# Projections of queries, keys and values by seven products of quarters, in steps on two shared PSUM banks

## The chip, the cores and the metric

The kernel runs on one core of a Trainium2 chip. Its metric is the device time of one execution in microseconds (us), the median of several. All arithmetic is in 32-bit floats. PE is the matrix engine, DVE the vector engine, ACT the scalar engine, POOL the GpSimd engine, SP the engine whose queue issues the DMAs.

## What is computed

Two blocks follow each other on 4 batches of 1024 rows of 512 features. The first is a graph attention over 20 neighbours. The second, which the change is in, is a transformer block with modulation by a condition vector:

```python
mod = silu(c) @ W_mod + b_mod
sh_msa, sc_msa, g_msa, sh_mlp, sc_mlp, g_mlp = split(mod, 6)
x = x + g_msa * attention(modulate(layernorm(x), sh_msa, sc_msa), W_qkv, W_out, b_out)
x = x + g_mlp * ff(modulate(layernorm(x), sh_mlp, sc_mlp), W1, b1, W2, b2)
```

`attention` projects the 512 features to queries, keys and values of 16 heads of 64, takes a softmax over all 1024 rows of the batch, and projects back with `W_out`. `ff` goes to 2048 hidden features, through an exact gelu, and back.

## The kernel before, in words

**Three stages.** The graph block runs first, over 32 tiles of 128 rows. Then the attention runs in 256 slots: 4 batches of 8 pairs of heads (`gp`) of 8 tiles of query rows. Then comes the feed-forward block. All instructions are issued in the order in which the program writes them, so each engine's queue is in program order.

**What a slot is.** Slot s handles one tile of 128 query rows for one pair of heads. Its fixed part is written first: `turn(s-1, 0)` (DVE transposes the weights of the slot before, in blocks of 32, into `wd`), `scores` (PE: four products, psc in two tiles of two PSUM banks), `largest` (DVE: the row maximum of both heads), `weights` (ACT: exponentials of both heads, with their sums), `scaled(0)` (ACT: first head's weights by the reciprocal of their sum), `turn(s-1, 1)`, `scaled(1)` (POOL: the second head's weights). After the fixed part, `emit(s, s+1)` writes what the planner has put into slot s, the fill. So on ACT every copy of the fill stands behind both exponentials and `scaled(0)` of the same slot, and on DVE every operation of the fill stands behind both maxima. The next slot's scores stand on PE behind the whole fill.

**The fill.** A list of entries `(lo, hi, units, place, function)`: a first and a last slot, a load of PE in units, and a place inside the slot. `attend` (weights times values for 256 queries, 2 units, place 1), the projections, `project` (1 unit, the product with `W_out`, added into the row by DVE) and `gates_of` (place 2), `norm_T` (transposes of normalised rows, place 3), and works of other engines without load. The planner starts each entry at its first slot and moves entries one by one to the slot of least load in their window while that lowers the load.

**The projections of before.** `mm_qk(b, gp, k, n, half)` makes half of a product of a [512 x 128] weight and the 512 x 512 half `n` of a batch's rows: two matmuls of 128x128 by 128x512. `mm_v(b, g, n)` makes 128 rows of values for a group of four heads: four matmuls of 128x128 by 128x256. Results go through four PSUM banks in turn (`MM`), which `attend`, `project`, `norm_T` and `gates_of` use too; ACT copies them to `qT`, `kT` (with its columns in another order) and `vt`. A matmul of 32-bit floats is two instructions in the profile. No projection waits in its slot for a copy that another entry of that slot has made.

**DMA.** `turn` on an odd slot issues four DMAs of 256 KB on SP's queue, which carry the tile `wd` (two slots' transposed weights of one head, two buffers per head) to `wT`.

**seven.** The feed-forward block already multiplies its quarters by seven products in place of eight (`seven`, `sums_a`, `sums_b`), on four banks. One of its units (`first`) is spread over the last slots of the attention, one step a slot.

Of the kernel before, what the change touches and what calls it, by code (L numbers as in the profile page):

```python
# [41 lines left out]
def cond_block_kernel(  # L42
# [49 lines left out]
    sel = cst.tile([P, B, P], F32, name="sel")  # L92
    for k in range(4):
        q = slice(32 * k, 32 * k + B)
        nc.vector.tensor_copy(sel[q], ident[q, q].unsqueeze(2).to_broadcast([B, B, P]))
# [23 lines left out]
    def spread(k, b, pg):  # L119

        q = slice(32 * k, 32 * k + B)
        nc.tensor.matmul(pg, lhsT=sel[q, b, :], rhs=gates[q, :], start=True, stop=True)
        return pg
# [6 lines left out]
    with ExitStack() as gctx:  # L130
# [16 lines left out]
        with ExitStack() as sctx:  # L147
# [58 lines left out]
            for b in range(B):  # L206
                pr = sps.tile([P, F], F32, name="pr", tag="s")
                nc.tensor.matmul(pr, lhsT=sel[:B, b, :], rhs=qrows, start=True, stop=True)
                evac(b, qrB[:, b, :], pr)
# [173 lines left out]
        def load_w(held, key, tag, src, cols):  # L383

            t = rp.tile([P, FC, 2, P], F32, name=tag, tag=tag, bufs=2)
            for k, col in enumerate(cols):
                nc.sync.dma_start(t[:, :, k, :], src[:, col : col + P].rearrange("(c p) f -> p c f", p=P))
            held[key] = t
# [58 lines left out]
        def seven(get, opens, short, lhs, rhs, nk, room, done):  # L447
# [5 lines left out]
            a, b, c, d, s5 = ({} for _ in range(5))  # L453

            def product(t, which, fresh):
                for q in range(2):
                    for k in range(nk):
                        nc.tensor.matmul(  # L458
                            t[:, q * HB : (q + 1) * HB],
                            lhsT=lhs(which, q, k),  # L460
                            rhs=rhs(which, k),
                            start=(fresh and q == 0 and k == 0),
                            stop=(k == nk - 1),
                            skip_group_check=True,
                        )

            def bank_of(held, name):
                held[0] = get(name)
                if opens and name in ("mb", "md"):
                    nc.tensor.matmul(held[0], lhsT=ident, rhs=hT[1, 0][:, 0, :], start=True, stop=True)  # L470
                return held[0]

            def step0():
                product(bank_of(a, "ma"), 0, True)
                nc.scalar.copy(bank_of(b, "mb"), a[0])  # L475

            def step1():
                product(bank_of(c, "mc"), 4, True)
                s5[0] = short()
                nc.scalar.copy(s5[0], c[0])  # L480

            def step2():
                product(b[0], 5, False)
                nc.vector.tensor_tensor(bank_of(d, "md"), b[0], s5[0], ALU.add)

            def step3():
                product(a[0], 1, False)
                done(0, 0, a[0])

            def step4():  # L490
                product(b[0], 6, False)
                s6 = room()
                nc.vector.tensor_tensor(s6, b[0], s5[0], ALU.add)
                done(1, 1, s6)

            def step5():
                product(d[0], 2, False)
                done(0, 1, d[0])

            def step6():  # L500
                product(b[0], 3, False)
                done(1, 0, b[0])

            return step0, step1, step2, step3, step4, step5, step6
# [3 lines left out]
        ex, hs, hx, tx = {}, {}, {}, {}  # L508

        def mlp_rows():  # L510

            h = hT[1, 0]
            if not tx:
                tx[0] = rp.tile([P, FC, VB * P], F32, name="tx", tag="hT", bufs=2)
            o = [tx[0][:, k, :].rearrange("p (c r) -> p c r", c=2) for k in range(3)]
            sums_b(nc.gpsimd, o, h[:, :2, :HB], h[:, :2, HB:], h[:, 2:, :HB], h[:, 2:, HB:])

        def mlp_weights(e, i, home):

            ex[i] = home()  # L520
            o = [ex[i][:, k * HB : (k + 1) * HB].rearrange("p (c f) -> p c f", c=2) for k in range(3)]
            w = w1g[i]
            sums_a(e, o, w[:, :2, 0, :], w[:, 2:, 0, :], w[:, :2, 1, :], w[:, 2:, 1, :])

        def up_lhs(p):
            def lhs(which, q, c):
                i = 2 * p + q
                at = {4: 0, 5: 1, 2: 2}.get(which)
                if at is not None:
                    return ex[i][:, at * HB + c * P : at * HB + (c + 1) * P]  # L530
                h, f = {0: (0, 0), 1: (0, 1), 3: (1, 1), 6: (1, 0)}[which]
                return w1g[i][:, 2 * f + c, h, :]

            return lhs

        def up_rhs(which, c):
            at = {4: 0, 5: 1, 3: 2}.get(which)
            if at is not None:
                return tx[0][:, at, c * HB : (c + 1) * HB]
# [253 lines left out]
        for s in range(-4, NTA + 2):  # L793
# [44 lines left out]
            if s == 25:  # L838
# [3 lines left out]
                load_v(0, 1)  # L842
# [5 lines left out]

    vp = ctx.enter_context(tc.tile_pool(name="vp", bufs=1, side="right", reuse_waits="tile"))
# [4 lines left out]
    with ExitStack() as actx:  # L854
        ap_ = actx.enter_context(tc.tile_pool(name="ap", bufs=1, reuse_waits="tile"))
        MM = dict(tag="mm", bufs=4)
# [45 lines left out]
        def mm_v(b, g, n):  # L902

            if (b, g) not in vt:
                vt[b, g] = vp.tile([P, NT, GW], F32, name="v", tag="v", bufs=2)
            if n % 2 == 0:
                part["v", n // 2] = ps.tile([P, 2, GW], F32, name="pvv", **MM)
            pt = part["v", n // 2]
            for c in range(FC):
                nc.tensor.matmul(  # L910
                    pt[:, n % 2, :],
                    lhsT=hT[0, 2 * b + n // VB][:, c, n % VB * P : (n % VB + 1) * P],
                    rhs=wv[b, g][:, c].rearrange("p k f -> p (k f)"),
                    start=(c == 0),
                    stop=(c == FC - 1),
                )
            if n % 2 == 1:
                nc.scalar.copy(vt[b, g][:, n - 1 : n + 1, :], pt)

        def attend(b, gp, k):  # L920
# [13 lines left out]
            if p == 0 and k == 0:  # L934
                oT[b, g] = op_.tile([P, 2, S], F32, name="oT", tag="oT", bufs=2)
            nc.scalar.copy(
                oT[b, g][:, p, k * QB : (k + 1) * QB].rearrange("p (t u q) -> p u t q", t=QT, u=4),
# [3 lines left out]
        def project(b, g, n):  # L941

            po = ps.tile([P, F], F32, name="pout", **MM)
            for p in range(2):
                nc.tensor.matmul(  # L945
                    po,
                    lhsT=oT[b, g][:, p, n * P : (n + 1) * P],
# [45 lines left out]
        def turn(b, gp, t, j):  # L993

            k, at = divmod(t, QT)
            if at == 0:
                wd[j] = ap_.tile([P, 4 * KC, QT, U], F32, name="wd", tag=f"wd{j}", bufs=2)
# [28 lines left out]

        def add(lo, hi, units, place, f, *args):
            fill.append((lo, hi, units, place, lambda: f(*args)))

        for b in range(B):  # L1030
            s0 = b * NP * NT
            for gp in range(NP):
                g, p = divmod(gp, 2)
                at = s0 + gp * NT
                if gp == 0 and b > 0:
                    for h, (ld, rws, tr) in enumerate(
                        ((-18, (-15, -14, -13, -12), -11), (-10, (-9, -9, -8, -8), -7))
# [6 lines left out]

                if at > 0:
                    for k in range(2):
                        for n in range(2):
                            for half in range(2):

                                lo = at - (8 if gp > 0 else (9, 5)[n])  # L1050
                                add(lo, at - (2 if gp < NP - 1 else 4), 1, 2, mm_qk, b, gp, k, n, half, bank)
                if p == 0:
                    for n in range(NT):
                        lo, hi = (at - 12, at + 1) if g > 0 else (max(at - (9, 5)[n // VB], 0), at + 3)
                        add(lo, hi, 1, 2, mm_v, b, g, n)
# [4 lines left out]
                if p == 1:  # L1060
                    for n in range(NT):
                        lo = at + QT * (NB - 1) + LAG + (3 if g == 0 else 2)
                        add(lo, lo + (7 if g == NGRP - 1 else 10), 1, 2, project, b, g, n)
# [11 lines left out]
                if at - 16 >= 0:  # L1075
                    add(at - 16, at - 16, 0, 0, load_qk, b, gp)
                if p == 0 and at - 24 >= 0:
                    add(at - 24, at - 24, 0, 0, load_v, b, g)
# [3 lines left out]
        add(NS - 18, NS - 18, 0, 0, norm_load, 1, 0)  # L1082
# [4 lines left out]
        for i, at in enumerate((NS - 14, NS - 11, NS - 13, NS - 12)):  # L1087
            add(at, at, 0, 0, load_w1, i, "wqk" if i < 2 else "wv")
        add(NS - 7, NS - 7, 0, 4, mlp_rows)
        for i in range(2):  # L1090
            add(NS - 9 + i, NS - 9 + i, 0, 4, mlp_weights, nc.gpsimd, i, home_q(("qT", "kT")[i]))

        def short():
            return op_.tile([P, F], F32, name="s", tag="s", bufs=2)
# [10 lines left out]
        first = seven(bank, True, short, up_lhs(0), up_rhs, 2, room0, done0)  # L1105
        for k, f in enumerate(first):
            at = NS - 7 + k
            add(at, at, (1.5, 1, 1.5, 1, 1, 1, 1)[k], 2, f)
# [3 lines left out]
        used = {}  # L1112
        for w, f in zip(where, fill):
            used[w] = used.get(w, 0) + f[2]
        moved = True
        while moved:
            moved = False
            for k, (lo, hi, units, _, _) in enumerate(fill):
                to = min(range(lo, hi + 1), key=lambda s: used.get(s, 0) - (units if s == where[k] else 0))
# [233 lines left out]
```

## Time and profile before

| | |
|---|---|
| median of three runs | 3174.8 us (3174.73 to 3180.2) |
| the profiled execution | 3184.05 us, of which the span from first to last instruction is 3182.3 us |
| PE busy | 3142.3 us, 99% of the span |
| DVE, ACT, POOL busy | 61%, 44%, 33% |
| graph block | first 457 us |
| attention slots | 457 us to 2350 us, 7.4 us a slot on average |
| feed-forward block | from 2390 us to the end |
| mean granted PE clock | 0.993 |

Busy time of PE is modelled from the start and the size of each matmul, and matmuls overlap in it, so a mean duration in a group is longer than the distance between two of them: busy time divided by the count is nearer to that distance. A line such as `L409 PE MATMUL pqk<-hT,wqk ... x1024 | 475.1, 604 | 0.0` gives the busy time, the mean of one instruction in ns, and the idle time of the engine before the group.

### The profile page before, as it was taken

The page shows a single profiled execution, that of the slowest core. Times are in us where ns is not written, and L with a number is a line of the kernel's source. Part 1 is how long each engine was busy: PE and PEld are TensorE (multiplying, and loading weights), DVE is VectorE, ACT ScalarE, POOL GpSimd, SP SyncE. Part 2 cuts the span into 40 slices and gives each one's busy share as a digit, 9 for nine tenths or more (in the row PEclk, how much of TensorE's full clock was granted, in tenths as well). Part 3 has the DMA queues.
Part 4 walks back from the last instruction along what each step waited for, and adds up shares of the span by engine and source line. Part 5 has one row for each costly group of instructions (what it writes and reads, how often), then busy time and mean ns, then how long its engine had stood idle before and what let it go on. Part 6 is the DMA issues. An engine that isn't in the chain of part 4 may idle for free.

```text
span 3182.3 us, 39273 instructions
## 1 busy us (share of the span) xinstructions
PE 3142.3 (99%) x14571; PEld 1938.9 (61%) x14571; DVE 1941.9 (61%) x2718; ACT 1406.2 (44%) x2312; POOL 1066.0 (33%) x580
## 2 busy tenths in 40 slices
PE   8999999999999999999999999999999999999999
PEld 5666665544444544454544454544457888888888
DVE  2688866777767777767777767777864332223222
ACT  1344446555555555555555555555641221112211
POOL 1344325344343544343544343544432101111020
PEclk8999999999999999999999999999999999999999
DMA  4233317776777776777776777776862101101010
GB/s 164 71 102 98 119 45 184 160 177 153 175 170 180 177 177 154 175 170 180 178 177 154 176 171 179 178 176 147 193 162 88 40 27 40 40 14 40 27 40 14
DMA packets 272850, 405.29 MB, mean 127 GB/s; under 512 B 24660, under 2 KB 97424, under 8 KB 272660
## 3 DMA queue, kind: packets, MB, share of 16 engines
q1 hardware_dynamic: 272660, 402.78, 50.6%
q8 instruction: 116, 1.90, 0.2%
q14 instruction: 74, 0.61, 0.1%
HBM read 109.08 MB, written 25.17 MB: 42 GB/s over the span
## 4 chain that ended last, share of the span: by engine, by line
PE 86%; DVE 5%; SPq 2%; DMA 2%; issue 2%; POOL 2%; ACT 1%; POOLq 0%; DVEq 0%; ACTq 0%
PE psc L965 14%; PE pqk L409 14%; PE pav L927 12%; PE pvv L910 7%; PE pout L945 6%; PE mbd L458 5%; PE mbu L458 5%; PE mad L458 3%; PE mau L458 3%; PE pa L647 2%; PE pf L607 2%; PE mcd L458 2%; PE mdd L458 2%; SPq L1004 2%; PE mdu L458 2%
## 5 line engine op out<-in xcount | busy, mean ns | idle before, releaser
L991 POOL TENSOR_SCALAR w<-w,sm 128x1024 f32<-128x1024 f32 x256 | 730.5, 2853 | 1074.3 <-DVE sm L987 1074.3
L982 ACT ACTIVATE w<-psc,mx 128x1024 f32<-128x1024 f32 x512 | 570.7, 1115 | 769.3 <-DVE mx L976 768.8
L976 DVE TENSOR_REDUCE mx<-psc 128x1 f32<-128x1024 f32 x512 | 601.3, 1215 | 261.9 <-PE psc L965 260.0
L1000 DVE STREAM_TRANSPOSE wd<-w 128x1024 f32<-128x1024 f32 x512 | 633.9, 1238 | 143.4 <-ACT w L989 118.0
L965 PE MATMUL psc<-kT,qT 64*128 64x512 f32 x2048 | 517.1, 616 | 2.0 <-DVE xs L723 0.9
L409 PE MATMUL pqk<-hT,wqk 128*128 128x512 f32 x1024 | 475.1, 604 | 0.0
L927 PE MATMUL pav<-wT,v 128*64 128x256 f32 x4096 | 472.1, 382 | 1.1 <-DMA wT<-wd 0.8
L927 PEld LDWEIGHTS pav<-wT,v 128*64 128x64 f32 x4096 | 284.4, 137 | 226.8 <-issue 78.9
L965 PEld LDWEIGHTS psc<-kT,qT 64*128 64x128 f32 x2048 | 185.8, 186 | 273.7 <-issue 161.1
L409 PEld LDWEIGHTS pqk<-hT,wqk 128*128 128x128 f32 x1024 | 185.0, 189 | 246.8 <-issue 244.2
L989 ACT ACTIVATE w<-w,sm 128x1024 f32<-128x1024 f32 x256 | 291.1, 1137 | 0.0
L945 PE MATMUL pout<-wout,oT 128*128 128x512 f32 x512 | 243.2, 610 | 0.0
L910 PE MATMUL pvv<-wv,hT 128*128 128x256 f32 x1024 | 238.3, 384 | 0.0
L910 PEld LDWEIGHTS pvv<-wv,hT 128*128 128x128 f32 x1024 | 190.8, 190 | 66.3 <-issue 43.8
L442 POOL TENSOR_TENSOR tx<-hT 128x512 f32<-128x512 f32 x8 | 10.2, 1269 | 565.0 <-DVE hT L381 565.0
L945 PEld LDWEIGHTS pout<-wout,oT 128*128 128x128 f32 x512 | 90.0, 189 | 134.5 <-issue 118.2
L647 PE MATMUL pa<-kp,sfT 128*128 128x320 f32 x512 | 143.5, 433 | 1.4 <-ACT sfT L622 1.4
L475 ACT COPY mbu<-mau 128x512 f32<-128x512 f32 x30 | 17.1, 570 | 287.8 <-PE mau L458 287.8
L647 PEld LDWEIGHTS pa<-kp,sfT 128*128 128x128 f32 x512 | 94.8, 190 | 38.2 <-ACT sfT L622 1.9
L953 DVE TENSOR_TENSOR xr<-pout,xr 128x512 f32<-128x512 f32 x128 | 85.2, 676 | 51.6 <-PE pout L945 51.1
L607 PE MATMUL pf<-wx,xT 128*128 128x512 f32 x256 | 115.3, 593 | 0.3 <-DVE pf L589 0.3
L458 PE MATMUL mad<-w,hs 128*128 128x256 f32 x512 | 113.1, 379 | 0.0
(276 smaller groups left out, 3559.3 us busy)
## 6 DMA issues: line engine op xcount, KB each, us to landing
wT<-wd SPq DMA_DIRECT2D x1024, 256.0 KB
wqk<-in_w_qkv SPq DMA_DIRECT2D x64, 256.0 KB
xs<-in_x SPq DMA_DIRECT2D x36, 256.0 KB
x1d<-xs SPq DMA_DIRECT2D x32, 256.0 KB
xl<-x1d SPq DMA_DIRECT2D x32, 256.0 KB
wv<-in_w_qkv SPq DMA_DIRECT2D x32, 256.0 KB
xr<-x1d SPq DMA_DIRECT2D x32, 256.0 KB
wout<-in_w_out SPq DMA_DIRECT2D x16, 512.0 KB
```

What stands on the lines that cost most here:

```text
L409: nc.tensor.matmul(pt, lhsT=wqk[b, gp][:, c, k, :], rhs=hT[0, 2 * b + n][:, c, :], start=(c == 0), stop=(c == FC - 1),)
L458: nc.tensor.matmul(t[:, q * HB : (q + 1) * HB], lhsT=lhs(which, q, k), rhs=rhs(which, k), start=(fresh and q == 0 and k == 0), stop=(k == ...
L647: nc.tensor.matmul(pas[i][:, n, :HF], lhsT=sfT2[i][:, c, :], rhs=kp[:, b, c, n * HF : (n + 1) * HF], start=False, stop=(c == FC - 1), skip ...
L910: nc.tensor.matmul(pt[:, n % 2, :], lhsT=hT[0, 2 * b + n // VB][:, c, n % VB * P : (n % VB + 1) * P], rhs=wv[b, g][:, c].rearrange("p k f ...
L927: nc.tensor.matmul(po[j * D : (j + 1) * D, :], lhsT=vt[b, g][:, m, p * P + j * D : p * P + (j + 1) * D], rhs=w[:, j, :, m, :], start=(m == 0),
L945: nc.tensor.matmul(po, lhsT=oT[b, g][:, p, n * P : (n + 1) * P], rhs=wout[b, g][:, p, :], start=(p == 0), stop=(p == 1),)
L965: nc.tensor.matmul(sc[j][:, n * F : (n + 1) * F], lhsT=qT[b, gp][q, t * P : (t + 1) * P], rhs=kT[b, gp][q, n * F : (n + 1) * F], start=Tru ...
L976: nc.vector.tensor_reduce(mx, sc, axis=AX.X, op=ALU.max, negate=True)
L982: nc.scalar.activation(w, sc, AF.Exp, bias=mx, accum_out=sm)
L989: nc.scalar.mul(w, w, sm)
L991: nc.gpsimd.tensor_scalar(w, w, sm, None, ALU.mult)
L1000: nc.vector.transpose(wd[j][:, :, at, :], wn.pop((b, gp, t, j)).rearrange("p (m k) -> p m k", k=U))
```

## The change

The queries and keys of a pair of heads, and the values of a group, are now made by seven products of quarters each (`seven`). Sums of quarters of the weights (`weight_sums`, on POOL) and of the rows (`row_sums`, DVE and POOL) are made beforehand. A unit of queries and keys is 7 steps of two matmuls of 128x128 by 128x512; a unit of values is 7 steps of eight matmuls of 128x128 by 128x128. All units of the attention and the feed-forward's first unit go through the same two PSUM banks, `q1` and `q2`; `attend`, `project`, `norm_T` and `gates_of` keep two banks in place of four. The steps of all units form one chain in a fixed order:

```diff
+        q1, q2 = (ps.tile([P, F], F32, name=n, tag=n) for n in ("q1", "q2"))
+        two_banks = {"ma": q2, "mb": q1, "mc": q1, "md": q2}
-        MM = dict(tag="mm", bufs=4)
+        MM = dict(tag="mm", bufs=2)
...
+            def start_d():
+                nc.vector.tensor_tensor(d, b, s5[0], ALU.add)
+            def step_a():
+                product(a, 0, True)
+                nc.scalar.copy(b, a)
+            def step_c():
+                product(c, 4, True)
+                s5.append(short())
+                nc.scalar.copy(s5[0], c)
+            def step_b():
+                product(b, 5, False)
+                if not shared:
+                    start_d()
+            def step_a2():
+                product(a, 1, False)
+                done(0, 0, a)
+                if shared:
+                    start_d()
+            def step_b2():
+                product(b, 6, False)
                 s6 = room()
+                nc.vector.tensor_tensor(s6, view(b), view(s5[0]), ALU.add)
                 done(1, 1, s6)
+            def step_d():
+                product(d, 2, False)
+                done(0, 1, d)
+            def step_b3():
+                product(b, 3, False)
+                done(1, 0, b)
+            return (*((step_c, step_a) if shared else (step_a, step_c)), step_b, step_a2, step_b2, step_d, step_b3)
...
+        def qk_steps(b, gp):
+            def room():
+                return keys_at(b, gp, 1)
+            def done(i, j, t):
...
+                if i == 0:
+                    nc.scalar.mul(qT[b, gp][:, j * F : (j + 1) * F], t, float(D**-0.5))
+                elif j == 0:
+                    nc.scalar.copy(keys_at(b, gp, 0), keys_of(t))
...
+        def v_steps(b, g):
...
+            def done(i, j, t):
+                if (i, j) != (1, 1):
+                    nc.scalar.copy(at(i, j), rows_of(t))
...
-                wd[j] = ap_.tile([P, 4 * KC, QT, U], F32, name="wd", tag=f"wd{j}", bufs=2)
+                wd[j] = ap_.tile([P, 4 * KC, QT, U], F32, name="wd", tag=f"wd{j}", bufs=1 + j)
...
-            t = rp.tile([P, FC, 2, P], F32, name=tag, tag=tag, bufs=2)
+            t = rp.tile([P, FC, 2, P], F32, name=tag, tag=tag, bufs=1 if tag == "wv" else 2)
...
+        def add_steps(lo, hi, units, steps, first=(0, 0, 1, 1, 2, 2, 3), last=(0, 1, 1, 2, 2, 3, 3)):
+            for f, a, z in zip(steps, first, last):
+                chain.append(len(fill))
+                add(lo + a, hi + z, units, 2, f)
+        ORDER = (
+            ("qk", 0, -5, -5), ("v", 0, -2, 0), ("qk", 1, 1, 3), ("qk", 2, 8, 9), ("v", 1, 9, 15),
+            ("qk", 3, 16, 18), ("qk", 4, 24, 25), ("v", 2, 25, 31), ("qk", 5, 32, 35), ("qk", 6, 40, 43),
+            ("v", 3, 40, 45), ("qk", 7, 48, 48),
+        )
...
+                    add(lo - 3, lo - 3, 0, 4, qk_sums, b, n)
+                    add_steps(lo, hi, 1, qk_steps(b, n))
...
+        first_sums, more_sums = row_sums(0)
+        first_sums()
+        more_sums(nc.vector)
+        emit(-3, 0)
```

The planner now puts the chain into slots by a search (`order_chain`) that keeps its order and the windows and minimises the sum of the squared loads of the slots, up to four steps a slot; it says nothing of what a step waits for. It alternates four times with the old way for the other entries. The smaller parts of the change: the first block's one-hot table `sel` becomes a broadcast of the identity; `oT` is one tile per pair of heads in three buffers; the feed-forward's first weights are loaded into buffers of the attention and their sums are made on POOL in the last slots; its openings of banks are left out, and its second bias is added in one piece.

What the planner's rule gives for the second batch, entries with load only, worked out from the list above (c, a, b, a2, b2, d, b3 are the steps; A is `attend`, p `project`, T `norm_T`, g `gates_of`):

```
59 qk0 c a           | 60 A qk0 b         | 61 qk0 a2 b2 d, g     | 62 A qk0 b3
63 v0 c a b          | 64 A v0 a2         | 65 v0 b2 d b3         | 66 A qk1 c
67 qk1 a b a2        | 68 A p p           | 69 p, qk1 b2 d        | 70 A qk1 b3
71 p p p             | 72 A p             | 73 p, qk2 c a         | 74 A qk2 b
75 qk2 a2 b2 d       | 76 A qk2 b3        | 77 v1 c a             | 78 A v1 b
79 v1 a2 b2          | 80 A v1 d          | 81 v1 b3, qk3 c a     | 82 A qk3 b
83 qk3 a2 b2 d       | 84 A qk3 b3        | 85 p p p              | 86 A p
87 p p p             | 88 A               | 89 qk4 c a b          | 90 A qk4 a2
91 qk4 b2 d b3       | 92 A p             | 93 v2 c a             | 94 A v2 b
95 v2 a2 b2          | 96 A v2 d          | 97 v2 b3, qk5 c       | 98 A qk5 a
99 qk5 b a2 b2       | 100 A p p          | 101 qk5 d b3, p       | 102 A p
103 p p p p          | 104 A qk6 c        | 105 qk6 a b a2        | 106 A qk6 b2
107 qk6 d b3, v3 c   | 108 A v3 a         | 109 v3 b a2           | 110 A v3 b2
111 v3 d b3          | 112 A qk7 c        | 113 qk7 a b a2        | 114 A qk7 b2
115 qk7 d b3         | 116 A T T          | 117 p p T T           | 118 A p
119 p p p            | 120 A              | 121 p p T T           | 122 A T T
```

## The prediction

> **What bounds the kernel now.** I first read the page's busy shares and groups, then, asking the trace for matmuls with all shapes apart, the one matmul that has the new shape of the value steps. Columns after the bar: busy us, mean ns of one; then idle time before.
>
> ```profile
> PE 3142.3 (99%) x14571; PEld 1938.9 (61%) x14571; DVE 1941.9 (61%) x2718; ACT 1406.2 (44%) x2312; POOL 1066.0 (33%) x580
> ...
> L409 PE MATMUL pqk<-hT,wqk 128*128 128x512 f32 x1024 | 475.1, 604 | 0.0
> L910 PE MATMUL pvv<-wv,hT 128*128 128x256 f32 x1024 | 238.3, 384 | 0.0
> L711 PE MATMUL po<-vb,wT 128*128 128x128 f32 x320 | 41.0, 275 | 0.0
> ```
>
> PE is busy 99% of the span and has no idle time before the projections: in the attention slots PE sets the time, and a projection that PE does not make is time saved, as long as PE is not made to wait instead. So the next view is the timeline of one slot, the one that begins at 1210.92 us (start, duration, engine):
>
> ```profile
> 1210.92 1.99 PE L965 MATMUL psc<-kT,qT 64*128 64x512 f32 x8
> ...
> 1212.94 2.36 DVE L976 TENSOR_REDUCE mx<-psc 128x1 f32<-128x1024 f32 x2
> 1214.20 1.11 ACT L982 ACTIVATE w<-psc,mx 128x1024 f32<-128x1024 f32 x1 [3.74 <-DVE mx L976]
> ...
> 1215.39 1.11 ACT L982 ACTIVATE w<-psc,mx 128x1024 f32<-128x1024 f32 x1
> ...
> 1216.49 1.14 ACT L989 ACTIVATE w<-w,sm 128x1024 f32<-128x1024 f32 x1
> 1216.67 0.13 DVE L987 RECIPROCAL sm<-sm 128x1 f32<-128x1 f32 x1
> ...
> 1217.53 0.36 ACT L936 COPY oT<-pav 128x256 f32<-128x256 f32 x1
> ...
> 1218.37 1.99 PE L965 MATMUL psc<-kT,qT 64*128 64x512 f32 x8
> 1218.47 0.59 ACT L918 COPY v<-pvv 128x512 f32<-128x512 f32 x1 [0.58 <-PE pvv L910]
> ```
>
> Scores, maxima, two exponentials and the scaled weights follow each other with no slack, and the first copy of the fill starts 1217.53 - 1210.92 = 6.6 us after the slot's first score. The next slot's scores start at 7.4 us. On DVE the fill may begin after the second reciprocal, at 1216.67 + 0.13 - 1210.92 = 5.9 us. Before, this lateness costs nothing: no PE work needs a copy made in its own slot, and four banks hold what is waiting.
>
> From the starts of the score groups over all slots: a slot lasts 5.6 us with two units of fill, 7.3 to 7.4 with three, 9.15 with four. So the scores take 1.9 us and each unit 1.85: a second step starts 3.75 us into a slot without `attend`, a third at 5.6.
>
> The prices of the copies between steps, from the groups of ACT and DVE in the feed-forward, where `seven` already runs, and of the keys:
>
> ```profile
> L475 ACT COPY mbu<-mau 128x512 f32<-128x512 f32 x30 | 17.1, 570 | 287.8 <-PE mau L458 287.8
> L480 ACT COPY s<-mcu 128x512 f32<-128x512 f32 x30 | 17.6, 586 | 32.5 <-PE mcu L458 32.5
> L484 DVE TENSOR_TENSOR mdu<-mbu,s 128x512 f32<-128x512 f32 x30 | 21.0, 700 | 95.7 <-PE mbu L458 95.7
> L421 ACT COPY kT<-pqk 128x512 f32<-128x512 f32 x64 | 65.8, 1068 | 14.8 <-PE pqk L409 14.8
> ```
>
> Last, what a wait of PE does to its clock: three windows around the longest wait near the end of the attention (us, PE busy, ..., the granted clock after the POOL column).
>
> ```profile
> 2313.40:2315.40 2.00, 0.17 (x1) 0.00 (x0) 1.25 (x1) 0.84 (x2) 1.98 (x2) 1.00 0.84 262
> 2315.43:2316.75 1.32, 1.32 (x6) 1.19 (x7) 0.00 (x0) 0.00 (x0) 1.29 (x2) 1.00 1.01 213
> 2316.75:2320.17 3.42, 3.42 (x10) 1.57 (x10) 0.00 (x0) 0.59 (x1) 3.42 (x3) 0.50 0.78 211
> ```
>
> PE stood still for 1.9 us, and 1.3 us later its clock was at half for 3.42 us: 1.7 us of work lost on top of the wait.
>
> **PE's own work: -74 us.** Queries and keys: 16 matmuls per pair of heads become 14, over 32 pairs 64 fewer, 128 instructions. At 475.1 / 1024 = 0.464 us each: -59. Values: 512 matmuls of 256 columns become 16 x 56 = 896 of 128 columns, 1792 instructions. By L711's own price, 41.0 / 320 = 0.128 us, they cost 229 us in place of 238.3: -9. But L711 runs in groups of ten and pays a start for each; inside its groups the starts lie 112 ns apart, and inside L910's 216 ns, which makes 201 against 221: -20. I take -15, as the new groups have sixteen.
>
> One rule speaks against this: the Trainium skill, "TensorE: Matmul & The Clock Gate", section "Back-to-back issue gap", says that with a weight load for each matmul a 128-column matmul takes about 81 ns where its columns alone would give 56. By that ratio the value steps would take 1792 x 0.108 x 1.45 = 280 us, an estimate, 42 more than now; the row with the very shape (112 ns against half of 216) shows almost none of it.
>
> **Waits inside a slot: +211 us.** Two banks carry a whole unit, so a step often needs a copy of the step before. b needs ACT's copy of a; b2 needs a2's copy by ACT and then DVE's `start_d`; b3 needs DVE's sum after b2; c of the next unit needs ACT's copy of b3. The pairs c a, b a2, b2 d and d b3 need nothing of each other. The planner weighs only loads, and its list for slots 59 to 122 puts dependent steps into one slot. Their copies then stand on ACT behind the exponentials, so not before 6.6 us, and PE has nothing else queued that can pass: the next slot's scores stand behind. I add 0.15 us for each signal between engines.
> - a then b, alone (67, 105, 113): b starts at 6.6 + 0.57 + 0.15 = 7.3 in place of 3.75: 3.6 each. After c and a (63, 89): another 0.59, 7.9 in place of 5.6: 2.3 each.
> - a2 then b2 (61, 75, 79, 83, 95): 6.6 + 0.59 + 0.70 + 0.3 = 8.2 in place of 3.75: 4.45 each; with b ahead (99): 2.6.
> - b3 then c (81, 97): 6.6 + 0.59 + 0.15 = 7.35: 3.6 each; d b3 c (107) with the keys' copy of 1.07: 8.4 in place of 5.6: 2.8.
> - b2 d b3 (65, 91): DVE's sum from 5.9, 0.69 and 0.3: 6.9 in place of 5.6: 1.3 each.
>
> Together 10.8 + 4.6 + 22.3 + 2.6 + 7.2 + 2.8 + 2.6 = 53 us. The other batches have the same pattern but for their ends: times four, 211 us. Nothing can be late before these waits, so nothing hides them; a slot with such a pair lasts 9 to 12 us.
>
> **Two banks for the rest: +38 us.** The third `project` or transpose of a slot needs the first one's bank, which DVE empties from 5.9 us on: 5.9 + 0.68 (L953's 676 ns) + 0.2 = 6.8 in place of 5.6, 1.2 us in seven slots of the batch (71, 85, 87, 103, 117, 119, 121); 0.6 us in 116 and 122. That is 9.6 a batch, 38 in all.
>
> **One buffer for `wd` of the first head: +56 us.** In the trace the four DMAs of a `wd` tile land 7.1 to 8.5 us after its transpose (median 7.6), and the next tile's transpose starts 4.6 to 7.4 us after (median 5.7): without the second buffer DVE waits there about 2 us, one slot in two, with the next slot's maxima queued behind. After a slot of 7.4 us there are 1.4 us of slack before those maxima; after one of 5.6 there are none. So everything in the following slot is late by 0 to 2.4 us, and the 56 hard pairs (14 a batch, all but b2 d b3) lie mostly in those slots: 0 to 134 us; I take 1 us for each, as most follow a slot of 7.4.
>
> **Clock: +72 us.** All 56 hard waits are longer than the 1.9 us that halved the clock above; each can lose 1.7 us: 0 to 96. A wait of 1.9 us at 2387 us was followed by no such drop, so I take three in four.
>
> The rule on the same page, section "What's actually happening", that the clock falls after an idle window of about 3.4 us, would spare the waits of 2.3 to 2.8 us and give at most 40 x 1.7 = 68 us, an estimate; the row shows a shorter wait doing it.
>
> **What costs nothing.** Per unit ACT makes five copies in place of four (+0.6 us) and DVE two sums (+1.4 us): over 48 units 27 and 67 us on engines busy 1067 and 1380 of the 1893 us of the slots; covered by PE as long as they are not in a dependent pair. POOL gets 48 x 4 sums at 0.73 us (the feed-forward's sums of weights), 140 us on 817. If that cover were gone they would cost their own sum. At the start DVE's row sums (four of about 1.2 us) stand before the first maxima and the first step: +3 us; the openings of banks and the earlier weights of the feed-forward give about as much back.
>
> **Sum.** -74 + 211 + 38 + 56 + 72 = +303. From the profiled 3184: 3487. That execution is 9 us above the median of the three runs, so 3478 against 3174.8.
>
> **Rivals.** *The copies are in time:* if ACT's copies ended before PE comes to the dependent step, only the arithmetic would be left, 3175 - 74 = 3101. Place: ACT between the last copy and the next exponential, where it is idle 2.6 us or more in every slot. Against it: ACT's order in the timeline; the copies would have to pass the exponentials. It decides if the mean wait of the 56 pairs is below 74 / 56 = 1.3 us with no other cost. 6%; and 2% that waits and savings happen to cancel within 6 us, which is about what a measurement of this kernel can tell from no change (0.2%). *Waits alone:* neither the clock nor the buffer costs anything: -80 + 211 + 38 = +169, 3344. For it: the other wait of 1.9 us; longer slots give the DMAs more time. 12%. *Everything at its upper end:* -68 + 211 + 38 + 134 + 96 = +411, 3586; DVE, held by the buffer and by `start_d`, then sets the odd slots. For it: DMA moves 171 GB/s through the slots at a busy share of 0.72, so landings will hardly be faster. 16%. My forecast between these: 64%. That leaves both tails a little beyond the bounds; range 3335 to 3600. All slower cases together 92%.
>
> **What would show it.** Right: slots 61, 75, 83 of 11 us and more; PE idle before the steps b, b2 and c, released by ACT and DVE, some 200 us or more; a granted clock below 0.98 between 500 and 2500 us; PE's busy share under 95%; 896 instructions for queries and keys and 1792 of 128 columns at 0.11 to 0.13 us. Wrong: steps starting within 0.3 us of each other in those slots, then my reading of ACT's order is false; or waits that are there with the clock at 1.00.

## The result and the profile after

The changed kernel takes 3663.66 us (median of four, 3657.35 to 3672.52) against 3177.5 us of the kernel before (3174.73 to 3182.89): a ratio of 1.153, 95% interval 1.1499 to 1.156. It is 486 us slower; 303 were forecast, 3600 was the upper end of the range. The profiled execution took 3672.52 us, span 3670.8.

The page of the changed kernel, busy shares, clock row and the groups that answer to those of before (after the bar: busy us, mean ns of one; then idle time before it and what ended it):

```profile
PE 3265.3 (89%) x15211; PEld 2003.4 (55%) x15211; DVE 2008.1 (55%) x2810; ACT 1420.7 (39%) x2359; POOL 1210.6 (33%) x746
...
PEclk8999989999899889899899989998999999999999
...
L1077 DVE STREAM_TRANSPOSE wd<-w 128x1024 f32<-128x1024 f32 x512 | 633.4, 1237 | 316.0 <-DMA wT<-wd 240.2
L460 PE MATMUL q<-hT,wqk 128*128 128x512 f32 (+1 forms) x396 | 219.9, 685 | 92.5 <-DVE q L470 92.5
L460 PE MATMUL q<-tx,ex 128*128 128x512 f32 (+1 forms) x264 | 165.1, 761 | 108.3 <-ACT q L474 68.9
L460 PE MATMUL q<-wv,hT 128*128 128x128 f32 x768 | 110.7, 304 | 49.2 <-DVE q L470 49.2
```

First, PE fell from 99% to 89%: it now waits in front of the projections, which had no idle time at all. Second, DVE's transposes into `wd` wait 240.2 us for the DMA that empties the buffer. Third, eight slices of the attention stand at 8 in the clock row, where all stood at 9 before.

The waits of PE (line that waits, what ends the wait: us in total, times, the longest):

```profile
PE q L460 <- DVE q L470: 141.7, 27, 6.8
PE q L460 <- ACT q L474: 75.5, 17, 6.9
PE pout L1022 <- DVE xr L1030: 41.4, 19, 4.2
PE q L460 <- ACT v L988: 39.4, 9, 7.1
PE q L460 <- ACT kT L966: 19.9, 4, 5.2
```

L470 is `start_d`, which b2 needs; L474 is the copy of a (for b); L988 and L966 empty a bank for the next unit. The four rows on `q` come to 276 us in 57 waits, where 56 pairs had been counted.

Windows of the changed kernel, the slots and the rest (us, busy time of PE, PEld, DVE, ACT, POOL, then the granted clock, the busy share of the DMA engines and GB/s):

```profile
460.80:2834.00 2373.20, 2003.21 (x9404) 1004.66 (x9404) 1450.07 (x1836) 1080.43 (x1681) 967.39 (x529) 0.91 0.58 137
2834.00:3670.00 836.00, 822.53 (x3760) 703.06 (x3760) 254.36 (x418) 163.36 (x347) 86.77 (x65) 0.99 0.13 42
```

The loss lies in the slots: 2373 us, where they took 1893 before. Slot 75, which holds `qk2 a2 b2 d`, shows all its parts. Its timeline in the changed kernel (start, duration, engine; in brackets the idle time before and its releaser):

```profile
1157.41 1.99 PE L1042 MATMUL psc<-kT,qT 64*128 64x512 f32 x8
...
1159.33 1.98 PE L460 MATMUL q<-hT,wqk 128*128 128x512 f32 x4
...
1160.91 1.25 DVE L1077 STREAM_TRANSPOSE wd<-w 128x1024 f32<-128x1024 f32 x1 [4.40 <-DMA wT<-wd]
1162.08 2.31 DVE L1053 TENSOR_REDUCE mx<-psc 128x1 f32<-128x1024 f32 x2
...
1165.59 1.14 ACT L1066 ACTIVATE w<-w,sm 128x1024 f32<-128x1024 f32 x1
...
1166.63 0.58 ACT L964 ACTIVATE qT<-q 128x512 f32<-128x512 f32 x1
1167.24 0.70 DVE L470 TENSOR_TENSOR q<-q,s 128x512 f32<-128x512 f32 x1 [1.34 <-ACT qT L964]
...
1168.09 3.75 PE L460 MATMUL q<-hT,wqk 128*128 128x512 f32 x4 [6.78 <-DVE q L470]
...
1174.57 1.99 PE L1042 MATMUL psc<-kT,qT 64*128 64x512 f32 x8
```

The slot lasts 1174.57 - 1157.41 = 17.16 us; three units of fill took 7.4 before. The maxima begin 4.67 us into the slot. In the slot that was shown of before they begin at 2.02, so the transpose that waits for its buffer makes the whole softmax 2.65 late. Step b2 begins at 10.68; without the 2.65 that is 8.03, and the prediction said 8.2. Then b2 and d take 1174.57 - 1168.09 = 6.48 us for 8 instructions, where 3.71 at 0.464 each were due: 2.77 lost to the clock. Together 7.4 + (8.03 - 3.75) + 2.65 + 2.77 = 17.1. The clock in this slot, by the windows of the same kernel:

```profile
1160.90:1164.40 3.50, 0.41 (x1) 0.00 (x0) 3.48 (x3) 1.11 (x2) 0.00 (x0) 0.89 0.92 205
1164.40:1167.90 3.50, 0.00 (x0) 0.00 (x0) 2.02 (x4) 2.81 (x6) 1.90 (x1) 0.50 0.05 14
1167.90:1171.40 3.50, 3.31 (x4) 1.51 (x5) 0.04 (x1) 0.00 (x0) 0.94 (x1) 0.50 0.02 5
1171.40:1174.57 3.17, 3.17 (x6) 1.01 (x4) 2.11 (x2) 0.00 (x0) 0.00 (x0) 0.61 0.00 0
```

The start of b2 was forecast to within 0.2 us of what is left without the buffer; the buffer had been priced at 1 us for such a pair and the clock at 1.3.

Below, "lost to the clock" is the busy time of PE in the stretches at a clock of 0.50, halved, after the first 60 us: 8.5 us before, 168.9 after.

### The profile page after: what moved, and what is told of

It is laid out like the page before. It is cut to its first block, busy times and chain, and to the rows that moved or that the text cites. A ratio compares the mean times of both kernels' runs of the same rounds, so it can differ in the third digit from the quotient of the medians.

```text
span 3670.8 us, 40854 instructions
## 1 busy us (share of the span) xinstructions
PE 3265.3 (89%) x15211; PEld 2003.4 (55%) x15211; DVE 2008.1 (55%) x2810; ACT 1420.7 (39%) x2359; POOL 1210.6 (33%) x746
## 4 chain that ended last, share of the span: by engine, by line
PE 52%; DVE 14%; DMA 11%; ACT 11%; SPq 7%; issue 4%; POOL 2%; DVEq 0%; POOLq 0%; ACTq 0%
DMA wT<-wd 11%; PE q L460 9%; ACT w L1059 6%; SPq L1081 6%; PE psc L1042 6%; DVE wd L1077 6%; PE mbd L460 5%; PE pav L1004 4%; PE mbu L460 4%; DVE mx L1053 4%; PE mad L460 3%; PE mau L460 3%; PE pout L1022 3%; ACT w L1066 2%; PE pa L677 2%
## 5 line engine op out<-in xcount | busy, mean ns | idle before, releaser
L1077 DVE STREAM_TRANSPOSE wd<-w 128x1024 f32<-128x1024 f32 x512 | 633.4, 1237 | 316.0 <-DMA wT<-wd 240.2
L1042 PE MATMUL psc<-kT,qT 64*128 64x512 f32 x2048 | 562.0, 643 | 24.1 <-ACT w L1059 17.1
L1042 PEld LDWEIGHTS psc<-kT,qT 64*128 64x128 f32 x2048 | 198.7, 197 | 325.5 <-issue 202.3
L460 PE MATMUL q<-hT,wqk 128*128 128x512 f32 (+1 forms) x396 | 219.9, 685 | 92.5 <-DVE q L470 92.5
L1022 PE MATMUL pout<-wout,oT 128*128 128x512 f32 x512 | 255.0, 636 | 41.4 <-DVE xr L1030 41.4
L460 PE MATMUL q<-tx,ex 128*128 128x512 f32 (+1 forms) x264 | 165.1, 761 | 108.3 <-ACT q L474 68.9
L460 PEld LDWEIGHTS q<-hT,wqk 128*128 128x128 f32 x396 | 83.0, 223 | 215.3 <-issue 213.7
L460 PEld LDWEIGHTS q<-tx,ex 128*128 128x128 f32 x264 | 56.9, 237 | 183.7 <-issue 176.5
L460 PE MATMUL q<-wv,hT 128*128 128x128 f32 x768 | 110.7, 304 | 49.2 <-DVE q L470 49.2
L460 PEld LDWEIGHTS q<-wv,hT 128*128 128x128 f32 x768 | 103.0, 216 | 63.9 <-issue 60.0
L474 ACT COPY mbu<-mau 128x512 f32<-128x512 f32 x30 | 17.1, 570 | 286.7 <-PE mau L460 286.7
```

The costliest lines, as they stand in the source:

```text
L460: nc.tensor.matmul(t[:, q * width : (q + 1) * width], lhsT=lhs(which, q, k), rhs=rhs(which, q, k), start=(fresh and q == 0 and k == 0), st ...
L1022: nc.tensor.matmul(po, lhsT=oT[b, 2 * g + p][:, n * P : (n + 1) * P], rhs=wout[b, g][:, p, :], start=(p == 0), stop=(p == 1),)
L1042: nc.tensor.matmul(sc[j][:, n * F : (n + 1) * F], lhsT=qT[b, gp][q, t * P : (t + 1) * P], rhs=kT[b, gp][q, n * F : (n + 1) * F], start=Tru ...
L1077: nc.vector.transpose(wd[j][:, :, at, :], wn.pop((b, gp, t, j)).rearrange("p (m k) -> p m k", k=U))
```

## The experiments

**Three buffers of `wd` shared in turn, where one head had one and the other two (e1).** The memory stays the same, so this takes the suspected wait away and nothing else.

```diff
-    wd[j] = ap_.tile([P, 4 * KC, QT, U], F32, name="wd", tag=f"wd{j}", bufs=1 + j)
+    wd[j] = ap_.tile([P, 4 * KC, QT, U], F32, name="wd", tag="wd", bufs=3)
```

> The changed kernel with the three buffers of wd shared by both heads in turn (one tag, three buffers) in place of one for the first head and two for the second; the memory is the same. Theory A (the held vector queue and the waits inside a slot feed each other): the vector engine's 236 us of waits for the DMAs of wd go to under 30, the copies in the following slot come earlier by what they were held, and the time falls by about 160 us to some 3500. Theory B (the sizes of the prediction were right for the buffer, and the miss is the clock alone): it falls by about 56 us, to some 3605. Theory C (the vector engine's wait is covered, and only the dependent steps cost): under 20 us.

Measured: 3486.53 us, ratio to before 1.098 (1.0957 to 1.1002). That is 177 us for the buffer, against 56 in the sum, and near Theory A's 160. PE's three largest waits in this kernel, and what is left of DVE's waits for the buffer:

```profile
PE q L460 <- DVE q L470: 105.7, 27, 4.3
PE q L460 <- ACT q L474: 53.9, 17, 3.6
PE q L460 <- ACT v L988: 30.4, 9, 3.5
...
DVE wd L1077 <- DMA wT<-wd: 2.6, 3, 0.9
```

The same 27, 17 and 9 waits are there, shorter by 67 us, and the time lost to the clock falls by 65 (168.9 to 103.5). All 57 waits before the steps now come to 201 us. Slot 75 in this kernel:

```profile
1101.62 1.99 PE L1042 MATMUL psc<-kT,qT 64*128 64x512 f32 x8
...
1103.64 2.36 DVE L1053 TENSOR_REDUCE mx<-psc 128x1 f32<-128x1024 f32 x2 [1.31 <-PE psc L1042]
...
1109.70 3.75 PE L460 MATMUL q<-hT,wqk 128*128 128x512 f32 x4 [4.17 <-DVE q L470]
```

The maxima begin 2.02 us into the slot, as before the change, and b2 begins at 8.08.

**An order in which no step needs a copy of its own slot (e2).** The search may no longer put two steps into one slot if they are one of the pairs a and b, a2 and b2, b2 and b3, b3 and the next c; b2 and b3 is the pair in "b2 d b3" of the prediction.

```diff
+        LATE = {(1, 2), (3, 4), (4, 6), (6, 0)}
...
+            if any(((n + k) % 7, (n + m - 1) % 7) in LATE for k in range(m - 1)):
+                break
```

> The changed kernel with one rule more in the planner: two steps of which the second needs a copy made after the first (a then b, a2 then b2, b2 then b3, b3 then the next unit's c) are not put into one slot. All else, the two banks too, is as in the change. Theory A and theory B alike: the waits of PE before the steps, some 280 us, nearly go, with most of the time at half clock: 3360 to 3400. Theory D (the price is in the steps themselves: narrow matmuls, more starts, two banks that are handed on): the waits move to other slots and the time stays within 40 us of 3664.

Measured: 3376.25 us, 1.0634 (1.0596 to 1.0672), 287 us less. The waits in front of the steps are gone (0.2 us is left on `q`); what is left on PE are waits for the exponentials and for DVE to empty the banks of `project`, and DVE still waits for the buffer. PE's two largest waits and DVE's first in this kernel:

```profile
PE psc L1042 <- ACT w L1059: 57.0, 46, 3.8
PE pout L1022 <- DVE xr L1030: 45.7, 19, 3.5
...
DVE wd L1077 <- DMA wT<-wd: 276.1, 87, 5.1
```

**Both edits together (e3).**

> Both edits together: the planner's rule and the three shared buffers of wd. Theory A: about 440 us less than the changed kernel, some 3220, with the waits for banks of project and of the transposes left (about 50 us) and short slots. Theory B: 211 + 72 + 56 = 339 less, some 3325.

Measured: 3201.98 us, 1.008 (1.0065 to 1.0095). With the new order the buffer costs 3376.25 - 3201.98 = 174 us, with the old 177; the order costs 285 with three buffers and 287 without. So the two costs add up, within the scatter of these runs (the four of the new order alone spread over 22 us). Together they are all but 24 us of the loss.

**The clock by itself (e4).** Ahead of each dependent step PE gets four, two or one more matmuls, whose results nobody reads, so that it waits less idly.

```diff
+        def keep_busy(n):
+            t = bank("idle")
+            for _ in range(n):
+                nc.tensor.matmul(t, lhsT=ident, rhs=gates, start=True, stop=True)
...
+                        if any(j - i < 7 and (i % 7, j % 7) in LATE for i in now_):
+                            keep_busy(1 if j % 7 == 6 else 4 if len(now_) == 1 else 2)
```

> The changed kernel with matmuls that nothing reads (the identity by 512 columns, one to four of them) on a spare bank of project in front of each step that waits for a copy made in its own slot, so that PE does not stand still there; results are as before. The waits stay. Theory A: the loss to the half clock, 169 us by the trace, goes by two thirds or more: 3500 to 3560, mean granted clock above 0.97. Theory B (the clock costs the 72 us of the prediction): some 3590. Theory E (the half clock falls into waits and costs nothing): 3660 or more.

Measured: 3588.74 us, 1.1304 (1.1287 to 1.1322): 75 us faster though PE does more. The time lost to the clock falls by 83 (168.9 to 85.9): by half, not by the two thirds of Theory A, whose range is missed. The time is that of Theory B, but 86 us lost to the clock are still there, so this run doesn't decide whether they count.

The same matmuls on top of the three shared buffers (e7) do:

> e1 (shared buffers of wd, the order as in the change) with the unread matmuls of e4 in front of the waiting steps; there the waits have the lengths that the prediction worked out, so the unread matmuls nearly fill them. Theory A (a us lost to the half clock is a us of time): of e1's 103 us of loss at least 75 go, 3487 to some 3400, clock above 0.98. Theory E (most of the half clock falls where PE would wait anyway): above 3450.

Measured: 3388.72 us, 1.0664 (1.0642 to 1.0686): 98 us below the kernel with the three buffers alone, and 86 less lost to the clock (103.5 to 17.1). Its mean clock, from the view of the cores:

```profile
core 0: 3389.2 us, clock 0.992
```

That is the clock of before (0.993), while the kernel is still 6.6% slower. The gain is more than the 72 us that Theory B of the last run had for all of the clock. So lost clock turns into time about one to one, and the waits themselves are the larger part.

**The single buffer alone, on the kernel before (e8).** Nothing of the seven products is in it.

```diff
-    wd[j] = ap_.tile([P, 4 * KC, QT, U], F32, name="wd", tag=f"wd{j}", bufs=2)
+    wd[j] = ap_.tile([P, 4 * KC, QT, U], F32, name="wd", tag=f"wd{j}", bufs=1 + j)
```

> The kernel before with one buffer of wd for the first head, nothing else of the change. Theory A (the held vector queue costs by itself: maxima, exponentials, then the next scores, and the banks that project waits for): 60 to 170 us more than before's 3176, the vector engine's waits for the DMAs of wd above 150 us in place of 15. Theory B (as in the prediction: it costs only where a step needs a copy of its own slot, and before has none): under 15 us more.

Measured: 3301.87 us, 1.0391 (1.0373 to 1.0409): 124 us, in a kernel without one dependent pair. DVE's largest wait and PE's largest in this kernel; before, they were 14.8 us in 17 waits and 0.8 us in 2:

```profile
DVE wd L1000 <- DMA wT<-wd: 478.5, 118, 5.4
...
PE psc L965 <- ACT w L982: 22.0, 23, 2.8
```

A DVE wait of 478.5 / 118 = 4.05 us in nearly every second slot holds the maxima: in the odd slots they begin 4.06 us after the first score (median), 2.02 before. The exponentials come late, and the next scores start late or sit half done. The distances between PE's starts show it: inside the groups of scores they add up to 440.6 us, 366.6 before, and those from the work ahead to a slot's first score to 136.5, 113.2 before. That is 97 of the 116 us by which the slots of the two profiled executions differ; another 10 lie inside the groups of `project`. Of the 124 us, 18.5 are lost to the clock (27.0 against 8.5 before).

**Fewer users of the two banks in a slot (e5).** On top of both edits, the planner counts `attend`, `project`, transposes and gates in a slot and pays 4 units for each beyond two.

```diff
+    return used.get(s, 0) + add_ * units + 4 * max(0, users.get(s, 0) + add_ * own - 2)
```

> e3 with one more rule: the planner counts what needs one of the two shared banks in a slot (attend, project, the transposes, the gates) and moves a third one elsewhere in its window, if it can. Theory A: of the time that e3 still loses, the waits for banks (in the slots project's starts lie 38 us further apart than before, the transposes' 9 us) go by some 30 us: about 3170, within 0.3% of before. Theory D (the two banks of the steps are the price): within 8 us of e3's 3202.

Measured: 3179.67 us, 0.9996 (0.9982 to 1.0011): level with before. The sum of distances between the starts in the groups of `project` is 219.1 us, as before (219.3); it was 257.0 with both edits alone. The transposes paid more than they did: 41.4, where it was 22.4 with both edits alone and 13.8 before.

**Other windows for the units, on top of that (e6).**

```diff
-            ("qk", 0, -5, -5), ("v", 0, -2, 0), ("qk", 1, 1, 3), ("qk", 2, 8, 9), ("v", 1, 9, 15),
+            ("qk", 0, -4, -4), ("v", 0, -2, 0), ("qk", 1, 1, 4), ("qk", 2, 8, 10), ("v", 1, 14, 16),
...
```

> e5 with other windows in ORDER, chosen so that the loads of the slots are more even under the rules of e2 and e5. Theory A: 10 to 15 us below e5, some 3157, 0.6% faster than before: what is left is the arithmetic (70 us less by the starts in e3) less short slots, the row sums at the start and some waits. Theory D: as e3 or slower.

Measured: 3189.74 us, 1.0032 (1.0018 to 1.0045). A miss: it is slower than the kernel it was to improve. Among PE's waits in it one has grown, from 2.7 us in one wait:

```profile
PE psc L1042 <- ACT kT L966: 14.4, 7, 2.9
```

A unit that ends one slot later than the old window allowed leaves its keys' copy on ACT when the first scores that read them are due.

**Transposes of normalised rows through the two banks of the steps (e9),** on top of the counted users. They lie in slots in which no unit is open, so `q1` and `q2` are free there; the planner then does not count them as users.

```diff
+        bank_q = (lambda name: q1, lambda name: q2)
-                            add(at + tr + c // 2, at + tr + c // 2, 0.4, 3, norm_T, 0, 2 * b + h, c, bank)
+                            add(at + tr + c // 2, at + tr + c // 2, 0.4, 3, norm_T, 0, 2 * b + h, c, bank_q[c % 2])
...
```

> e5 with the transposes of norm_T on the two banks of the steps, which no step uses in those slots, in place of the two banks of attend and project; the planner no longer counts the transposes among the users of those. Theory A: in e5 the transposes' starts lie 28 us further apart in sum than before, with PE waiting for project's bank; that goes, and project may stand beside them: about 28 us below e5, some 3150, 0.9% faster than before. Theory D (the steps on two banks cannot gain more than their own starts and waits cost): within 8 us of e5.

Measured: 3155.8 us (3151.16 to 3159.54), 0.9928 (0.9916 to 0.9941): 0.7% below before. This and the next are the fastest that were found. In the slots of this kernel PE has its clock again (windows, the same columns):

```profile
457.00:2330.00 1873.00, 1856.73 (x9408) 978.68 (x9409) 1448.07 (x1840) 1080.95 (x1686) 967.50 (x530) 1.00 0.73 173
```

**Both: transposes and other windows (e10),** the windows now chosen so that keys are ready in time.

> e9 with windows in ORDER that make the slots' loads more even, and that end each unit of keys two slots before its first use (e6's ended later: the scores waited 14 us for the copy of the keys). Theory A: up to 7 us below e9, 3143 to 3150. Otherwise windows are worth nothing beyond e9.

Measured: 3155.41 us, 0.9927 (0.9913 to 0.994): nothing beyond the kernel above. The wait for the keys is back at 2.7 us, so the windows of e6 had caused it, but evener loads brought nothing.

## Why the direction was right and the size was not

| step of the sum | forecast | measured | from |
|---|---|---|---|
| PE's own work | -74 | about -70 | distances of starts in the projections: 681.5 before, some 612 for the same work with both edits |
| waits inside a slot | +211 | +193 | 3486.53 - 3201.98 = 285, less 92 lost to the clock (103.5 - 11.9) |
| two banks for the rest | +38 | +47 | both edits against before: `project` +38, transposes +9 |
| one buffer for `wd` | +56 | +112 | 3663.66 - 3486.53 = 177, less 65 lost to the clock |
| clock | +72 | +157 | 92 with the order, 65 with the buffer |
| not in the sum | 0 | about +49 | both edits: scores +28, weights times values +10, the rest partly in the start and the clock |
| sum | +303 | +488 | 486 by the times |

**Right: the arithmetic.** Steps of 128 columns start 112 ns apart (median in the changed kernel), about half of the 216 ns of 256 columns before. The Trainium skill, "TensorE: Matmul & The Clock Gate", section "Back-to-back issue gap", has about 81 ns for 128 columns where the columns alone would give 56. Such a ratio was not seen in these 32-bit matmuls.

**Right: the dependent pairs.** The reading of ACT's order (first copy of the fill 6.6 us into a slot) gave b2 at 8.2 where slot 75 has 8.08 with three buffers, and 211 for all where 193 were measured as time and 201 as waits. With its clock the order was to cost 283 and cost 285; that this comes so close is luck, since the waits were 18 less than forecast and their clock 20 more (92 for 72). Every wait before the steps left when the order was changed, so the rival in which the copies are in time is out.

**Right: the banks,** 38 for 47; the planner that counts users brought the 38 of `project` back.

**Failed: the step on the one buffer for `wd`.** It said that everything in the following slot is late by 0 to 2.4 us, and then charged 1 us to each of the 56 hard pairs, and nothing to any other slot, for which it gives no reason but 1.4 us of slack after a slot of 7.4. The run with the single buffer on the kernel before tells against that: 124 us without any pair. The landings were read rightly (the next write of the same buffer comes 8.0 us after the last, in place of 5.7, so 2.3 late); what was wrong is who pays. Every second slot pays, some 106 / 118 = 0.9 us on average in the kernel before, and slot 75, with a dependent pair, pays 2.65. In the changed kernel itself the slots of the profiled executions grow by 182 us against three buffers, clock included: by 93 among the steps, where the sum had looked, but by 43 at the scores and 38 at `project` and the transposes, where it had nothing. The upper bound of 134 held the 112 us of waiting.

**Failed with it: the clock.** The clock was counted once for each pair, at 1.7 us at most, from one stretch of 3.42 us at half clock. In the changed kernel 27 stretches last 3.41 us, but 42 last 6.83 and 5 last 10.24: 157 us more are lost than with both edits, where the bound was 96. Even with three buffers 15 of the stretches last 6.83, and the order alone loses 92 us where 72 were put down. A wait that the buffer makes longer loses more: slot 75 stood for 6.78 us and lost 2.77, since the clock was still at 0.50 up to 1171.40 and at 0.61 on average after it. And the softmax that comes late brings waits of its own. So the buffer lost 65 us to the clock that had no place in the sum.

The Trainium skill, "TensorE: Matmul & The Clock Gate", section "What's actually happening", has the clock fall after an idle window of about 3.4 us. That would have made the term smaller still. In the kernel before with the single buffer only one wait of PE behind the start of the kernel reaches 3.4 us, yet the clock is halved in twelve stretches, five before. One case (PE's timeline, then the window behind the wait, clock 0.51):

```profile
1288.16 2.66 PE L945 MATMUL pout<-wout,oT 128*128 128x512 f32 x4 [1.93 <-ACT oT L936]
...
1289.30:1292.70 3.40, 3.40 (x8) 0.94 (x9) 1.84 (x2) 0.00 (x0) 3.25 (x3) 0.51 0.58 144
```

**Missing: the scores.** Distances inside the groups of scores grow from 366.6 us to 394.0 with both edits. Nearly all of it lies behind short slots: 83 slots are shorter than 6.5 us, 22 before, and the groups behind them take 1.76 us on average (1.55 before), the others 1.42 to 1.45 in both kernels. The likely reason is that a short slot leaves less time for the exponentials, and the next scores wait for their banks; it was not tried by itself.

**The rivals.** "Waits alone" fell at 3344, since both the clock and the buffer cost; "everything at its upper end", 3586, was nearest, and rightly put the weight on DVE and the buffer. It was still 78 us short: its clock ended at 96 where 157 were lost, and it had nothing for the scores. What was said to show the forecast right was there: slots 61, 75 and 83 of 16.2, 17.2 and 13.2 us, 276 us of waits before the steps, a clock of 0.91 in the slots, 89% for PE.

**Open.** One buffer costs 174 to 177 us here and 124 on the kernel before, also with no pair in a slot. The distances between PE's starts tell where it falls: with the new order 130 us at the scores and 43 at `project` and the transposes, on the kernel before 97 and 10. So the two banks that `project` and the transposes have left are likely a part of the 50 us. Why the scores pay more was not settled. Of the 50, 25 are clock (44.0 against 18.5), which these distances include.

## What to carry to other kernels

Price a buffer that is taken away on the kernel without the rest of the change: if DVE or ACT stands still in it, everything behind it in that queue is late, wherever it stands still, and not only where something new depends on it. When a step needs a copy from another engine, look at what stands ahead of that copy in its queue and put the step into the next slot; here a rule of a few lines in the planner was worth 285 us. Where a wait can't be moved, add to it the work that follows at half clock, and don't take the shortest stretch for all of them.

## What the runs showed of the hardware

Filling PE's waits with matmuls that nobody reads made the kernel faster, by 75 and 98 us, close to the 83 and 86 us that were no longer lost to the clock. Stretches at half clock lasted 3.41, 6.83 or 10.24 us, and a wait of 1.9 us could bring one. And matmuls of 128 columns in 32 bits cost about half of those of 256 (112 against 216 ns) when sixteen instructions follow each other.
